# A product of halves split once more: three of seven sub-products in seven half-width ones, mask stores on another queue, the stage in written order

## The chip, the cores and the metric

The kernel runs on one core of a Trainium2 chip. The metric is device time in microseconds; times are medians of several runs. The engines are TensorE (PE, with its weight loads shown as PEld), VectorE (DVE), ScalarE (ACT), GpSimd (POOL) and SyncE (SP, which here only issues DMAs). L12 is line 12 of the kernel.

## The reference, cut to what matters

Two graph layers on x (4096 x 512) and adj (4096 x 4096), each added to its input and normalized over the row. The second layer contains the product that is changed:

```python
x = layernorm(x + relu(adj @ (max(sign(x), 0) @ sign(w0).T)))      # layer 0
node_att = softmax(x @ node_w, axis=0)
h = x @ edge_w                                                     # the changed product
e = where(adj > 0, h @ h.T, NEG_BIG)
edge_att = softmax(e, axis=1)
x = layernorm(x + (adj * (node_att * edge_att)) @ (x @ w1) + bias) # layer 1
```

All is float32. Adjacency is symmetric in its pattern, about 1.6% filled, so `adj > 0` is a mask of the score matrix.

## The kernel before, in words

The kernel goes through four large stages: the aggregation of layer 0 (L459, L460, from 55 to 505 us), the product h (505 to 602 us), the scores h h^T with their masks and exponentials, and the aggregation of layer 1 (L1413, L1563). TensorE does their matmuls nearly without a pause.

In the stage of h, x1T holds the normalized rows transposed (512 features on four chunks of 128 partitions, 4096 columns), and the result is hT, laid out in the same way. Both are cut into quarters: two halves of the features (`HK` = 2 chunks each) and two halves of the columns (g and g + `HG`, 512 columns of one block each). So for each of four g a 2 x 2 block product is computed with seven sub-products in place of eight (Strassen's scheme in Winograd's form). Their left operands are sums of quarters of edge_w, made once on GpSimd (`lops`, L480 to 483: s1 to s4); their right operands are x1T's quarters and four differences of them, t1 to t4, made on VectorE (L498, 499, 502, 504), each 128x1024.

`seven` (L90) does one g: each sub-product m is two feature blocks q times two chunks k of 128, four matmul instructions of 128x128 by 128x512 into a PSUM bank per q. A float32 matmul instruction runs as two passes through the array, so TensorE's rows count passes. Six PSUM banks are held, three pairs. The order of sub-products is 0, 5, 4, 6, 1, 3, 2. ScalarE copies the first and fifth out (L113, L127), VectorE adds the others into hT (L116, L122, L123, L131, L135). A scheduler orders these instructions by its own costs in this stage.

Between sub-products `between_h` steps the remaining work of other stages along:

- `late`: the rest of the last node blocks of layer 0, with their Strassen operands for a later stage, written to DRAM by GpSimd's queue (L388 to 414). The last block's normalization (L356 to 367) and its transposes (TensorE L419, copied by ScalarE L420) fall into the first microseconds of the product.
- `rights_h`: the t differences of the next g.
- `premask`: the adjacency's masks. A piece is loaded from adj (SyncE's queue, L345, 128x1024 float32, 512 KB), VectorE turns it into a bfloat16 mask in the same buffer (L339), and GpSimd's queue stores it in DRAM (L340, 256 KB), for the score stage to read. 26 of the pieces are left for this stage. They go through seven buffers (`single`, `ends`, four in `more`, `sums_l`), of which three are left free at a time (`ahead` = 3).

After the product in the code stand the node maximum (VectorE L534), the maximum across partitions (GpSimd L536), its negation, the exponential (ScalarE L540) and the sum across partitions (GpSimd L542). The scheduler moves them to 512 to 523 us. Then the score stage begins: VectorE forms operands from hT (`right`, L874 to 877; `lent` and `slot`, L783 to 796), TensorE multiplies (L745, L806).

Of the kernel before, what the change touches and what calls it, by code (L numbers as in the profile page):

```python
# [11 lines left out]
F32 = mybir.dt.float32  # L12
# [3 lines left out]
ALU = mybir.AluOpType  # L16
AX = mybir.AxisListType

P = 128
# [10 lines left out]
def kernel(  # L30
# [13 lines left out]
    nc = tc.nc  # L44
    N, D = x.shape
# [41 lines left out]

    xw = big.tile([P, NB, D], F32R, name="xw", tag="large")

    def seven(lop, rop, dests, after):  # L90

        K = len(rop(0))
        banks = [[ps_mm.tile([P, W], F32, name="seven", tag="mm") for q in range(2)] for _ in range(3)]

        def multiply(bank, m, first, then):
            for q in range(2):
                for k in range(K):  # L100
                    nc.tensor.matmul(  # L101
                        banks[bank][q],
                        lop(m, q)[k],
                        rop(m)[k],
                        start=(first and k == 0),
                        stop=(k == K - 1),
                        skip_group_check=not first,
                    )
                then(banks[bank][q], q, *dests[q])
                after(None, None)  # L110

        def m1(ps, q, c11, c12, c21, c22):
            nc.scalar.copy(c21, ps)  # L113

        def u2(ps, q, c11, c12, c21, c22):
            nc.vector.tensor_add(c12, c21, ps)  # L116

        def nothing(*_):
            pass

        def u3(ps, q, c11, c12, c21, c22):
            nc.vector.tensor_add(c22, c21, ps)  # L122
            nc.vector.tensor_add(c22, c22, banks[2][q])  # L123
            after(q, 3)

        def m2(ps, q, c11, c12, c21, c22):
            nc.scalar.copy(c11, ps)  # L127
            after(q, 0)

        def m4(ps, q, c11, c12, c21, c22):  # L130
            nc.vector.tensor_add(c21, c21, ps)  # L131
            after(q, 2)

        def m3(ps, q, c11, c12, c21, c22):
            nc.vector.tensor_add(c12, c12, ps)  # L135
            after(q, 1)

        multiply(0, 0, True, m1)
        multiply(1, 5, True, u2)
        multiply(2, 4, True, nothing)  # L140
        multiply(1, 6, False, u3)
        multiply(0, 1, False, m2)
        multiply(1, 3, False, m4)
        multiply(2, 2, False, m3)

    def layernorm(ts_):
        n = len(ts_)
# [11 lines left out]
    with (  # L159
# [65 lines left out]
        def product(g, j):  # L225
            pw = pws[g, j] = ps_mm.tile([P, D], F32, name="pw", tag="mm")
            for k in range(KD):
                nc.tensor.matmul(pw, rights_s[g][:, k, ts(j, P)], bw[:, k, :], start=(k == 0), stop=(k == KD - 1))
                if g == 0 and (not j or k == KD - 1):
                    zeros(2)  # L230
# [97 lines left out]
        bufs = deque([pair[:, 0, :], pair[:, 1, :], single, ends])  # L328
        loaded = deque()

        def premask(queue, left, ahead=2):

            if loaded and (len(bufs) <= ahead or len(pieces) == left):
                (r, j, c), a = loaded.popleft()

                m = a.bitcast(BF16).rearrange("p (c w) -> p c w", c=2)[:, :, :W]
                a_ = a.rearrange("p (c w) -> p c w", c=2)

                tc.keep_in_program_order(nc.vector.tensor_scalar(m, a_, 0.0, NEG_BIG, ALU.is_le, ALU.mult))  # L339
                nc.gpsimd.dma_start(mask_d[r][:, c : c + 2, j, :], m)  # L340
                bufs.append(a)
            if len(pieces) > left:
                r, j, c = pieces.popleft()
                a = bufs.popleft()
                queue.dma_start(a, adj[ts(r * BG + j, P), c * W : (c + 2) * W])  # L345
                loaded.append(((r, j, c), a))
# [83 lines left out]
        with tc.manual_schedule(engines={mybir.EngineType.DVE, mybir.EngineType.Activation}):  # L430
            for n in range(NB):
                b = n // 2 // BG * 2 * BG + n // 2 % BG + n % 2 * BG
                xb = rows.tile([P, D], F32, name="xb", tag="rows")
                nc.sync.dma_start(xb, x[ts(b, P), :])
                if b in early:

                    before = xb, rest(n, b, xb, accs[n], before and before[0])
                    if n == 0:
                        parts.append(before[1])
                    continue  # L440
                acc = ps_mm.tile([P, D], F32, name="acc", tag="mm")
                for half in range(2):
                    at = stream.tile([P, HB, P], F32, name="at", tag="stream")
                    nc.sync.dma_start(at, adj_t[b, :, ts(half, HB), :])

                    for q in range(2):
                        aq = at[:, ts(q, QC), :]
                        hi = sp.tile([P, QC, P], F32R, name="hi", tag="hi")
                        nc.scalar.copy(hi, aq)  # L449
                        lo = sp.tile([P, QC, P], F32R, name="lo", tag="lo")  # L450
                        nc.vector.tensor_sub(lo, aq, hi.bitcast(F32))  # L451
                        if n == 2 and half == 1 and q == 0:
                            parts.append(before[1])
                        step()
                        if half == 1:
                            premask(nc.scalar, 26)
                        for c in range(QC):
                            kb = half * HB + q * QC + c
                            nc.tensor.matmul(acc, hi[:, c, :], xw[:, kb, :], start=(kb == 0), stop=False)  # L459
                            nc.tensor.matmul(acc, lo[:, c, :], xw[:, kb, :], start=False, stop=(kb == NB - 1))  # L460
                parts.append(rest(n, b, xb, acc, before[0]))
                before = xb, None
                if n == NB - 3:
                    assert not loaded
                    bufs.clear()
                    bufs.extend((single, ends))
                    we_s = wp.tile([P, KD, D], F32, name="we_s")
                    nc.sync.dma_start(we_s, edge_w.rearrange("(k p) o -> p k o", p=P))
            while parts:
                step()  # L470
# [12 lines left out]
        nc.gpsimd.tensor_sub(s4, l12, s2)  # L483
        left_h = l11, l12, s4, l22, s1, s2, s3

        more = [stream.tile([P, 2, 2 * W], F32, name="more", tag="stream") for _ in range(2)]
        bufs.extend(m[:, n, :] for m in more for n in range(2))
        bufs.append(sums_l.rearrange("p n f -> p (n f)"))
        for _ in range(4):
            premask(nc.sync, 0, 3)  # L490
        count = [0]
        rights = {}

        def rights_h(g):
            r11, r12 = (x1T[:, :HK, ts(c, W)] for c in (g, g + HG))
            r21, r22 = (x1T[:, HK:, ts(c, W)] for c in (g, g + HG))
            t1, t2 = (sp.tile([P, HK, W], F32, name="t12", tag="hi") for _ in range(2))
            nc.vector.tensor_sub(t1, r12, r11)  # L498
            nc.vector.tensor_sub(t2, r22, t1)
            yield  # L500
            t3, t4 = (sp.tile([P, HK, W], F32, name="t34", tag="lo") for _ in range(2))
            nc.vector.tensor_sub(t3, r22, r12)
            yield
            nc.vector.tensor_sub(t4, r21, t2)
            rights[g] = r11, r21, r22, t4, t1, t2, t3
            yield

        ahead_h = deque(p for g in range(1, HG) for p in [rights_h(g)] * 3)
        for _ in rights_h(0):
            pass  # L510

        def between_h(q, n):
            count[0] += q is None
            if q is None and count[0] > 1:
                next(late[-1], None)
            if q is None and count[0] % 14 in (8, 10, 13) and ahead_h:
                next(ahead_h.popleft())
            if q is None and count[0] > 6 and count[0] % 5 % 2 == 0:
                premask(nc.sync, 0, 3)

        for g in range(HG):
            right_h = rights.pop(g)
            seven(
                lambda m, q: [left_h[m][:, k, ts(q, P)] for k in range(HK)],
                lambda m: [right_h[m][:, k, :] for k in range(HK)],
                [[hT[:, q + f, ts(c, W)] for f in (0, HK) for c in (g, g + HG)] for q in range(2)],
                between_h,
            )

        assert not loaded and not pieces  # L530


    nmax = const.tile([P, 1], F32, name="nmax")
    nc.vector.tensor_reduce(nmax, node_s, AX.X, ALU.max)  # L534
    gmax = const.tile([P, 1], F32, name="gmax")
    nc.gpsimd.partition_all_reduce(gmax, nmax, P, bass_isa.ReduceOp.max)  # L536
    nc.vector.tensor_scalar(gmax, gmax, -1.0, None, ALU.mult)
# [1416 lines left out]
```

## Time and profile before

| | us |
|---|---|
| runs | 1904.31, 1905.71, 1904.44 |
| median | 1904.44 |
| profiled execution | 1903.96 |
| its span | 1902.2 |
| TensorE busy | 1890.8 |
| stage of the changed product | 505.4 to 602.1 |

The profile is of one execution. The span counts from the first to the last instruction; 1.76 us of the execution's time lie around it. Rows name engine, line, operation, and the tiles written and read. [...]

### The profile page before, as it was taken

Reading aid. Unit: us, or ns where it says so; the run is one execution under the profiler, and the core shown is the slowest. Engines: PE = TensorE matmul, PEld = TensorE weight load, DVE = VectorE, ACT = ScalarE, POOL = GpSimd, SP = SyncE. Lnnn points to the kernel's source line nnn. Section 1 sums busy time; section 2 is a strip of 40 time slices with the busy share of each in tenths; the row PEclk is TensorE's granted clock in tenths of the full one; section 3 lists DMA queues with packets and bytes.
Section 4 is the critical chain, followed back from the end, with each engine's and each line's share of the span. In section 5 each row is a group of like instructions: output and inputs, shape, how many; then the busy total and the mean of one; then the engine's idle time right before and its main releaser. Section 6 shows DMA issues by size and latency. Waiting matters only on the chain.

```text
span 1902.2 us, 21262 instructions
## 1 busy us (share of the span) xinstructions
PE 1890.8 (99%) x7054; PEld 1263.4 (66%) x7054; DVE 1527.5 (80%) x2421; ACT 1024.6 (54%) x1669; POOL 314.1 (17%) x449
## 2 busy tenths in 40 slices
PE   9999999999999999999999999999999999999998
PEld 6888888888645656565667556666666666656646
DVE  7777677776877689888896887898879988898947
ACT  6433333333211567666777666665676567667732
POOL 0133132232331111111110111111111101110100
PEclk9999999999999999999999999999999999999999
DMA  9889898898585379577795978878777878787831
GB/s 321 299 322 362 308 339 323 330 353 321 179 295 190 141 267 346 191 259 277 286 334 166 327 279 297 287 288 300 273 278 287 294 270 277 268 318 253 286 114 56
DMA packets 143919, 521.00 MB, mean 274 GB/s; under 512 B 15040, under 2 KB 15040, under 8 KB 136128
## 3 DMA queue, kind: packets, MB, share of 16 engines
q1 hardware_dynamic: 64368, 235.43, 36.7%
q0 software_dynamic: 67632, 248.54, 34.2%
q10 hardware_dynamic: 11808, 35.66, 5.0%
q8 instruction: 56, 0.92, 0.2%
q14 instruction: 55, 0.45, 0.1%
HBM read 397.93 MB, written 121.63 MB: 273 GB/s over the span
## 4 chain that ended last, share of the span: by engine, by line
PE 89%; DVE 7%; ACT 2%; DMA 1%; issue 1%; ACTq 0%; SPq 0%; DVEq 0%
PE bank L1413 33%; PE acc L460 11%; PE acc L459 11%; PE bank L1011 11%; PE seven L101 5%; PE po L1563 4%; PE pt L707 3%; PE bank L806 2%; PE bank L970 2%; PE bank L933 2%; PE bank L745 2%; DVE lent L1182 1%; PE pt L419 1%; DVE slot L1182 1%; PE acc L253 1%
## 5 line engine op out<-in xcount | busy, mean ns | idle before, releaser
L1413 PE MATMUL bank<-lent,lop 128*128 128x256 f32 (+1 forms) x1368 | 433.0, 466 | 1.1 <-DVE lent L1194 0.7
L459 PE MATMUL acc<-xw,hi 128*128 128x512 f32 x960 | 376.4, 392 | 0.0
L460 PE MATMUL acc<-xw,lo 128*128 128x512 f32 x960 | 374.2, 390 | 0.0
L1413 PEld LDWEIGHTS bank<-lent,lop 128*128 128x128 f32 x1368 | 259.3, 190 | 146.1 <-issue 119.9
L1413 PE MATMUL bank<-slot,lop 128*128 128x512 f32 (+1 forms) x928 | 335.4, 508 | 0.4 <-DMA lop<-lop_d 0.2
L1413 PEld LDWEIGHTS bank<-slot,lop 128*128 128x128 f32 x928 | 176.0, 190 | 136.8 <-issue 121.3
L449 ACT CAST hi<-at 128x1024 fp32r<-128x1024 f32 x120 | 126.5, 1054 | 203.2 <-PE acc L459 152.9
L1424 ACT COPY over<-bank 128x512 f32<-128x512 f32 x200 | 116.0, 585 | 198.1 <-PE bank L1413 194.5
L460 PEld LDWEIGHTS acc<-xw,lo 128*128 128x128 f32 x960 | 180.3, 188 | 37.1 <-DVE lo L451 0.3
L459 PEld LDWEIGHTS acc<-xw,hi 128*128 128x128 f32 x960 | 180.3, 188 | 36.8
L451 DVE TENSOR_TENSOR lo<-at,hi 128x1024 fp32r<-128x1024 f32 x120 | 147.8, 1232 | 64.6 <-ACT hi L449 64.1
L678 ACT ACTIVATE line<-line,nmax_c 128x512 f32<-128x512 f32 x160 | 115.2, 726 | 22.4 <-DVE nmax_c L669 22.0
L669 DVE CUSTOM_DVE_ANT_0 line<-lent,slot 128x512 f32<-128x512 bf16 x144 | 93.1, 687 | 9.5 <-ACT slot L708 6.8
L1575 DVE SCALAR_TENSOR_TENSOR xb<-po,f,xb 128x256 f32<-128x256 f32 x84 | 40.3, 481 | 75.0 <-PE po L1563 70.8
L1386 ACT COPY bank<-over 128x512 f32<-128x512 f32 x144 | 86.8, 603 | 0.0
L707 PEld LDWEIGHTS pt<-ident,lent 128*128 128x128 f32 x406 | 50.9, 141 | 36.6 <-issue 24.2
L745 PE MATMUL bank<-hT 128*128 128x512 f32 (+3 forms) x256 | 75.1, 433 | 0.0
L1182 DVE CUSTOM_DVE_ANT_1 lent<-lent,line 128x2048 f32<-128x2048 f32 x32 | 73.0, 2283 | 1.1 <-DMA lent<-s_d 1.1
L708 ACT COPY slot<-pt 128x512 f32<-128x512 f32 (+3 forms) x125 | 68.0, 554 | 10.8 <-PE pt L707 10.8
L420 ACT COPY x1T<-pt 128x512 f32<-128x512 f32 x32 | 18.8, 587 | 101.7 <-PE pt L419 101.7
L1188 ACT ACTIVATE slot<-slot 128x2048 f32<-128x2048 f32 x35 | 67.3, 1924 | 10.8 <-DMA slot<-in_adj_t_dram 10.8
L1182 DVE CUSTOM_DVE_ANT_1 slot<-slot,line 128x2048 f32<-128x2048 f32 x32 | 73.1, 2284 | 0.0
(356 smaller groups left out, 3280.1 us busy)
## 6 DMA issues: line engine op xcount, KB each, us to landing
lop<-lop_d SPq DMA_DIRECT2D x154, 512.0 KB, 4.4
at<-in_adj_t_dram SPq DMA_DIRECT2D x60, 1024.0 KB, 7.3
slot<-in_adj_t_dram POOLq DMA_DIRECT2D x37, 1024.0 KB, 8.1
s_d<-slot POOLq DMA_DIRECT2D x32, 1024.0 KB, 7.6
slot<-s_d POOLq DMA_DIRECT2D x31, 1024.0 KB, 7.4
lent<-s_d POOLq DMA_DIRECT2D x29, 1024.0 KB, 8.2
lent<-in_adj_t_dram POOLq DMA_DIRECT2D x27, 1024.0 KB, 7.6
lent<-in_adj_dram SPq DMA_DIRECT2D x48, 512.0 KB, 6.2
```

The source lines that it names most:

```text
L101: nc.tensor.matmul(banks[bank][q], lop(m, q)[k], rop(m)[k], start=(first and k == 0), stop=(k == K - 1), skip_group_check=not first,)
L449: nc.scalar.copy(hi, aq)
L451: nc.vector.tensor_sub(lo, aq, hi.bitcast(F32))
L459: nc.tensor.matmul(acc, hi[:, c, :], xw[:, kb, :], start=(kb == 0), stop=False)
L460: nc.tensor.matmul(acc, lo[:, c, :], xw[:, kb, :], start=False, stop=(kb == NB - 1))
L678: nc.scalar.activation(line, line, AF.Exp, bias=nmax_c[:, b, c : c + 1], scale=-1.0, accum_out=sum_c[:, b, c : c + 1])
L707: nc.tensor.transpose(pt[:, j, :], src[:, ts(j, P)], ident)
L745: nc.tensor.matmul(pe[:, lo * P :], hT[:, k, ts(A * BG + i, P)], hT[:, k, (B * BG + lo) * P : (B + 1) * W], start=(k == 0), stop=(k == KD ...
L1011: nc.tensor.matmul(ps, left[m][:, k, q, :], right[m][:, k, :], start=(first and k == 0), stop=(k == KD // 2 - 1), skip_group_check=not first,)
L1182: pinned[0](nc.vector._custom_dve(TENSOR_ADD_SAT, out=q, in0=q, in1=m, s0=0.0, s1=-HUGE))
L1413: nc.tensor.matmul(ps, lop[:, k, :], rop[:, k, :], start=start, stop=(k == K - 1), skip_group_check=True)
L1424: nc.scalar.copy(self.to(), self.bank[:, : self.w])
```

## The change

For the first g one of the seven sub-products (5), for the others three (0, 4 and 5), are themselves split into seven products by the same scheme: over the two chunks, the two feature blocks and two halves of 256 columns. Such a sub-product was four matmul instructions of 512 columns and is now seven of 256 (`quarters`). Its operands are made by GpSimd: `inner_left` (four 128x128 sums, once for each of the three left operands) and `inner_right` (four 128x256 sums, for each split sub-product). The partial products meet in PSUM: a small bank `own` (one of the two that the transposes use) holds two of them, ScalarE copies parts into the sub-product's banks and into a scratch tile (five copies of 128x256 for each split), and TensorE accumulates onto these copies; VectorE adds twice 128x256.

TensorE, VectorE and ScalarE follow the written order in this stage (`manual_schedule`). The instructions of split sub-products alternate with each other and with whole ones (`mix`), and the second half of the last sub-product is issued among the next g's first (`over`). The sub-products run in the order 0 and 4, 5 with 1, 2, 6, 3. t1 and t2 of the next g are made earlier than before.

Mask stores go to SyncE's queue, behind which the loads stand; four buffers (`more`) at first and `sums_l` from count 16, one of them left free at a time. The pieces go at counts 4, 5, 7, 12 and from then on at two of three counts; there are 12 counts for each g, 48 in all. `single` and `ends` are no longer mask buffers in this stage, and the two loads into them before it are gone.

The node maximum is taken at count 46; what hangs on it stays behind the product in the code. In the order of the built program, the two `right` subtractions that ran before the end of the stage stand behind it.

The diff, cut to its core:

```diff
-    def seven(lop, rop, dests, after):
+    def seven(lop, rop, dests, after, inner, spare, over):
...
+        def quarters(bank, m, z):
+            left, right = inner[m]
+            own = ps_tr.tile([P, W], F32, name="own", tag="tr")
+            y = own[:, :HD]
+            alone_ = z is None
+            z = own[:, HD:] if alone_ else z
+            (x11, x12), (x21, x22) = ((x[:, :HD], x[:, HD:]) for x in banks[bank])
+            zs = spare()
+
+            def multiply(ps, n, first=False):
+                nc.tensor.matmul(ps, left[n], right[n], start=first, stop=True, skip_group_check=True)
+
+            multiply(y, 0, True)
+            if not alone_:
+                nc.scalar.copy(x11, y)
+            yield
+            multiply(z, 4, not alone_ and bank == 0)
+            if alone_:
+                nc.scalar.copy(x11, y)
+            yield
+            multiply(y, 5)
+            nc.scalar.copy(x12, y)
+            nc.scalar.copy(zs, z)
+            yield
+            multiply(y, 6)
+            nc.scalar.copy(x22, y)
+            nc.scalar.copy(x21, y)
+            yield
+            multiply(x11, 1)
+            yield
+            multiply(x12, 2)
+            nc.vector.tensor_add(x12, x12, zs)
+            yield
+            multiply(x21, 3)
+            nc.vector.tensor_add(x22, x22, zs)
+            yield
...
-        multiply(0, 0, True, m1)
-        multiply(1, 5, True, u2)
-        multiply(2, 4, True, nothing)
-        multiply(1, 6, False, u3)
-        multiply(0, 1, False, m2)
-        multiply(1, 3, False, m4)
-        multiply(2, 2, False, m3)
+        if 0 in inner:
+            z = [banks[1][0][:, h * HD : (h + 1) * HD] for h in range(2)]
+            order = (0, 1, 0, 1, 2, 0, 1, 2, 0, 1, 0, 1, 0, 1, 0, 1)
+            mix(order, quarters(0, 0, z[0]), quarters(2, 4, z[1]), over[0])
+        else:
+            alone(product(0, 0, True, nothing))
+            alone(product(2, 4, True, nothing))
+        for q, (c11, c12, c21, c22) in enumerate(dests):
+            nc.scalar.copy(c21, banks[0][q])
+        for q, (c11, c12, c21, c22) in enumerate(dests):
+            nc.vector.tensor_add(c22, c21, banks[2][q])
+        mix((0, 0, 1, 0, 1, 1, 0, 0, 0, 1, 0), quarters(1, 5, None), product(0, 1, False, m1))
+        for q, (c11, c12, c21, c22) in enumerate(dests):
+            nc.vector.tensor_add(c12, c21, banks[1][q])
+        alone(product(2, 2, False, m2))
+        alone(product(1, 6, False, m6))
+        over[0] = product(1, 3, False, m3)
+        next(over[0])
+        next(over[0])
+        after()
...
-                nc.gpsimd.dma_start(mask_d[r][:, c : c + 2, j, :], m)
+                (to or nc.gpsimd).dma_start(mask_d[r][:, c : c + 2, j, :], m)
...
+        def inner_right(R, *to):
+            r11, r12, r21, r22 = (R[:, k, ts(c, HD)] for k in range(2) for c in range(2))
+            t1, t2, t3, t4 = to
+            nc.gpsimd.tensor_sub(t1, r12, r11)
+            nc.gpsimd.tensor_sub(t2, r22, t1)
+            nc.gpsimd.tensor_sub(t4, r21, t2)
+            nc.gpsimd.tensor_sub(t3, r22, r12)
+            return r11, r21, r22, t4, t1, t2, t3
...
-        bufs.append(sums_l.rearrange("p n f -> p (n f)"))
-        for _ in range(4):
-            premask(nc.sync, 0, 3)
+        for _ in range(3):
+            premask(nc.sync, 0, 1, nc.sync)
...
-            if q is None and count[0] % 14 in (8, 10, 13) and ahead_h:
-                next(ahead_h.popleft())
-            if q is None and count[0] > 6 and count[0] % 5 % 2 == 0:
-                premask(nc.sync, 0, 3)
+            if g + 1 < HG:
+                if n == 4:
+                    rights[g + 1].make(1)
+                    inside(g + 1, 0, rights[g + 1].r11)
+                    inside(g + 1, 4, rights[g + 1].t[1])
+                elif n == 7 + 3 * (not g):
+                    rights[g + 1].make(2)
+                    inside(g + 1, 5, rights[g + 1].t[2])
+                elif n == 11:
+                    rights[g + 1].make(3)
+            if n == 2 and 0 < g:
+                rights[g].make(4)
+            if count[0] == 12 * HG - 2:
+                nc.vector.tensor_reduce(nmax, node_s, AX.X, ALU.max)
+            if count[0] in (4, 5, 7, 12) or count[0] > 12 and count[0] % 3:
+                premask(nc.sync, 0, 1, nc.sync)
...
+        with tc.manual_schedule(engines={mybir.EngineType.DVE, mybir.EngineType.Activation, mybir.EngineType.PE}):
...
-    nmax = const.tile([P, 1], F32, name="nmax")
-    nc.vector.tensor_reduce(nmax, node_s, AX.X, ALU.max)
```

More of the change, by code (lines that the diff above doesn't have):

```diff
@@ L88, with product @@
     xw = big.tile([P, NB, D], F32R, name="xw", tag="large")
-    def seven(lop, rop, dests, after):
+    def seven(lop, rop, dests, after, inner, spare, over):
         K = len(rop(0))
         banks = [[ps_mm.tile([P, W], F32, name="seven", tag="mm") for q in range(2)] for _ in range(3)]
-        def multiply(bank, m, first, then):
+        def product(bank, m, first, then):
             for q in range(2):
+                ps = banks[bank][q]
                 for k in range(K):
                     nc.tensor.matmul(
[L102 to L107, printed above, removed]
-                    )
[L109 to L116, printed above, removed]
+                        ps, lop(m, q)[k], rop(m)[k], start=(first and k == 0), stop=(k == K - 1), skip_group_check=not first
+                    )
+                    if k == K - 1:
+                        then(ps, *dests[q])
+                    yield
[32 more added lines that the diff above has]
+            nc.vector.tensor_add(x22, x22, zs)
+            yield
@@ L118, in nothing, with mix @@
         def nothing(*_):
             pass
[L121 to L126, printed above, removed]
+        def mix(order, *gens):
+            gens = [list_ for list_ in gens]
+            for n, k in enumerate(order):
+                next(gens[k])
+                if n % 4 == 3:
+                    after()
+            for gen in gens:
+                assert next(gen, None) is None
+            if len(order) % 4 > 1:
+                after()
@@ L127, in m2, with alone, m1, m6 @@
+        def alone(gen):
+            for n, _ in enumerate(gen):
+                if n % 2:
+                    after()
+        def m1(ps, c11, c12, c21, c22):
             nc.scalar.copy(c11, ps)
-            after(q, 0)
-        def m4(ps, q, c11, c12, c21, c22):
+        def m6(ps, c11, c12, c21, c22):
+            nc.vector.tensor_add(c22, c22, ps)
+        def m3(ps, c11, c12, c21, c22):
             nc.vector.tensor_add(c21, c21, ps)
-            after(q, 2)
-        def m3(ps, q, c11, c12, c21, c22):
+        def m2(ps, c11, c12, c21, c22):
@@ L135, in m3 @@
             nc.vector.tensor_add(c12, c12, ps)
-            after(q, 1)
-        multiply(0, 0, True, m1)
-        multiply(1, 5, True, u2)
-        multiply(2, 4, True, nothing)
-        multiply(1, 6, False, u3)
-        multiply(0, 1, False, m2)
-        multiply(1, 3, False, m4)
-        multiply(2, 2, False, m3)
+        if 0 in inner:
[5 more added lines that the diff above has]
+            alone(product(2, 4, True, nothing))
@@ L146, in layernorm @@
+        over[0] = product(1, 3, False, m3)
+        next(over[0])
+        next(over[0])
+        after()
     def layernorm(ts_):
@@ L329, with premask @@
         loaded = deque()
-        def premask(queue, left, ahead=2):
+        def premask(queue, left, ahead=2, to=None):
             if loaded and (len(bufs) <= ahead or len(pieces) == left):
@@ L465 @@
                     bufs.clear()
-                    bufs.extend((single, ends))
                     we_s = wp.tile([P, KD, D], F32, name="we_s")
@@ L484, with inner_left @@
         left_h = l11, l12, s4, l22, s1, s2, s3
+        def inner_left(L, to):
+            l11, l21, l12, l22 = (L[:, k, ts(f, P)] for k in range(2) for f in range(2))
+            s1, s2, s3, s4 = (to[:, n, :] for n in range(4))
+            tc.keep_in_program_order(nc.gpsimd.tensor_add(s1, l21, l22))
+            nc.gpsimd.tensor_sub(s2, s1, l11)
+            nc.gpsimd.tensor_sub(s3, l11, l21)
+            tc.keep_in_program_order(nc.gpsimd.tensor_sub(s4, l12, s2))
+            return l11, l12, s4, l22, s1, s2, s3
@@ new lines, in inner_right, with row_halves @@
+        def inner_right(R, *to):
[6 more added lines that the diff above has]
+            return r11, r21, r22, t4, t1, t2, t3
+        def row_halves():
+            x = rows.tile([P, D], F32, name="right_i", tag="rows")
+            return [x[:, ts(n, HD)] for n in range(2)]
@@ L486 @@
+        ends_i = wp.tile([P, 4, HD], F32, name="ends_i", tag="ends")
+        to_i = {0: [ends_i[:, n, :] for n in range(4)]}
+        mixed = wp.tile([P, 4 * P + 2 * HD], F32, name="mixed", tag="quarter", bufs=2)
+        lefts_i = {5: inner_left(s2, mixed[:, : 4 * P].rearrange("p (n f) -> p n f", f=P))}
+        inners = [{} for _ in range(HG)]
         more = [stream.tile([P, 2, 2 * W], F32, name="more", tag="stream") for _ in range(2)]
         bufs.extend(m[:, n, :] for m in more for n in range(2))
-        bufs.append(sums_l.rearrange("p n f -> p (n f)"))
@@ L489 @@
-        for _ in range(4):
-            premask(nc.sync, 0, 3)
+        for _ in range(3):
+            premask(nc.sync, 0, 1, nc.sync)
         count = [0]
[L492 to L514, printed above, removed]
-                next(late[-1], None)
-            if q is None and count[0] % 14 in (8, 10, 13) and ahead_h:
-                next(ahead_h.popleft())
-            if q is None and count[0] > 6 and count[0] % 5 % 2 == 0:
-                premask(nc.sync, 0, 3)
[L521 to L528, printed above, removed]
+        over = [None]
@@ new lines, with __init__, make, of @@
+        nmax = const.tile([P, 1], F32, name="nmax")
+        class Rights:
+            def __init__(self, g):
+                self.r11, self.r12 = (x1T[:, :HK, ts(c, W)] for c in (g, g + HG))
+                self.r21, self.r22 = (x1T[:, HK:, ts(c, W)] for c in (g, g + HG))
+                self.t = {}
+            def make(self, n):
+                tag = "hi" if n < 3 else "lo"
+                t = self.t[n] = sp.tile([P, HK, W], F32, name="t12" if n < 3 else "t34", tag=tag)
+                a, b = {
+                    1: (self.r12, self.r11),
+                    2: (self.r22, self.t.get(1)),
+                    3: (self.r22, self.r12),
+                    4: (self.r21, self.t.get(2)),
+                }[n]
+                nc.vector.tensor_sub(t, a, b)
+            def of(self, m):
+                return (self.r11, self.r21, self.r22)[m] if m < 3 else self.t[4 if m == 3 else m - 3]
@@ new lines, with inside @@
+        rights = [Rights(g) for g in range(HG)]
+        for n in (1, 2, 3, 4):
+            rights[0].make(n)
+        to_i[5] = row_halves() + row_halves()
+        inners[0][5] = lefts_i[5], inner_right(rights[0].t[2], *to_i[5])
+        to_i[4] = [mixed[:, 4 * P + n * HD : 4 * P + (n + 1) * HD] for n in range(2)] + row_halves()
+        zs_ = deque((wp.tile([P, HD], F32, name="z_s", tag="scr"), wp.tile([P, HD], F32, name="z_s", tag="warm")))
+        def inside(g, m, R):
+            inners[g][m] = lefts_i[m], inner_right(R, *to_i[m])
@@ new lines, in between_h @@
+        def between_h():
+            count[0] += 1
+            g, n = divmod(count[0], 12)
+            if count[0] > 6:
+                next(late[-1], None)
+            if count[0] == 16:
+                assert next(late[-1], None) is None
+                bufs.append(sums_l.rearrange("p n f -> p (n f)"))
+            if count[0] == 1:
+                for m, x, tag in ((0, l11, "nw_b"), (4, s1, "bias_b")):
+                    to = wp.tile([P, 4, P], F32, name="left_i", tag=tag)
+                    lefts_i[m] = inner_left(x, to)
+            if g + 1 < HG:
[14 more added lines that the diff above has]
+                premask(nc.sync, 0, 1, nc.sync)
@@ new lines @@
+        with tc.manual_schedule(engines={mybir.EngineType.DVE, mybir.EngineType.Activation, mybir.EngineType.PE}):
+            for g in range(HG):
+                right_h = rights[g]
+                seven(
+                    lambda m, q: [left_h[m][:, k, ts(q, P)] for k in range(HK)],
+                    lambda m, r=right_h: [r.of(m)[:, k, :] for k in range(HK)],
+                    [[hT[:, q + f, ts(c, W)] for f in (0, HK) for c in (g, g + HG)] for q in range(2)],
+                    between_h,
+                    inners[g],
+                    lambda: zs_.rotate() or zs_[0],
+                    over,
+                )
+            for _ in over[0]:
+                pass
```

## The prediction

> **What bounds the kernel now.** I read the page first, then the chain of waits around the stage, then windows of 12 us, then what the stage's own matmuls waited for. The page:
>
> ```profile
> PE 1890.8 (99%) x7054; PEld 1263.4 (66%) x7054; DVE 1527.5 (80%) x2421; ACT 1024.6 (54%) x1669; POOL 314.1 (17%) x449
> ```
>
> TensorE is busy for all but 1902.2 − 1890.8 = 11.4 us of the span, so only less matmul work can help, and whatever makes TensorE wait costs in full. The chain of waits, from 495 to 640 us:
>
> ```profile
> 505.37 4.29 PE seven L101 x10
> 509.78 0.63 PE pt L419 x4
> 510.41 88.42 PE seven L101 x206
> 598.92 0.54 issue
> 599.46 1.22 DVE right L874
> ```
>
> The columns are start, length, what and how many. The product runs from 505.4 to 602.1 us with one interruption, the four transposes of the last node block. The chain leaves TensorE at 598.9 only because the next stage's first operands hang on VectorE. Windows (busy time of PE, PEld, DVE, ACT, POOL, then granted clock, DMA share, GB/s):
>
> ```profile
> 517.00:529.00 12.00, 12.00 (x29) 5.32 (x28) 11.32 (x22) 2.87 (x5) 6.59 (x9) 1.00 0.40 122
> 541.00:553.00 12.00, 12.00 (x29) 5.32 (x28) 9.12 (x13) 1.17 (x2) 2.18 (x3) 1.00 0.95 354
> 589.00:602.00 13.00, 13.00 (x31) 5.70 (x30) 7.09 (x10) 1.17 (x2) 1.28 (x3) 1.00 0.06 20
> 602.00:615.00 13.00, 13.00 (x55) 8.84 (x54) 13.00 (x31) 3.42 (x9) 0.00 (x0) 1.00 0.84 322
> ```
>
> PE is full in every one, at the full clock. VectorE is nearly full early in the stage (11.32 of 12), has room later, and is full without a gap for 13 us after it. The mask traffic is squeezed into 525 to 585 us. 28 weight loads in 12.00 us give 0.4286 us a pass; each matmul instruction is two passes, 0.857 us.
>
> **Part 1, the product itself.** Before, 4 × 7 × 2 × 2 = 112 matmul instructions, 112 × 0.857 = 96.0 us. After, the first g splits one product and the others three: 72 full instructions and 10 × 7 = 70 of half the columns. The price of a half comes from a later stage that has both widths:
>
> ```profile
> 1540.94 1.03 PE L1563 MATMUL po<-over 128*128 128x256 f32 x4
> 1541.81 1.03 PE L1413 MATMUL bank<-slot,lop 128*128 128x256 f32 x4
> 1542.67 1.89 PE L1413 MATMUL bank<-lent,lop 128*128 128x256 f32 x8
> 1544.40 1.03 PE L1413 MATMUL bank<-slot,lop 128*128 128x256 f32 x4
> ```
>
> From 1540.94 to 1545.26 (where the next row starts) there are 20 passes, 0.216 us each, half of 0.43; the weight load, 0.190 us, still fits below, with 26 ns to spare. So 72 × 0.857 + 70 × 0.432 = 61.7 + 30.2 = 91.9 us: **−4.1 us**, 0.21% of the run. That is all that the change can bring; 0.2% (3.8 us, about what a measurement of this kernel can tell from no change) is passed only if nearly nothing is lost.
>
> **Part 2, what it adds on the other engines.** ScalarE gets 10 × 5 = 50 copies of 128x256, 0.36 us each: 18 us against 1.17 of 12 busy, covered. Inside a split product the second use of a half bank waits for the copy of the first (0.36 us); other products' matmuls, 0.43 to 0.86 us each, lie between, so nothing, or 0.36 us plus a semaphore once per split (4 us over ten) without that cover; I take 0.2. VectorE gets 20 PSUM adds of 128x256 at 0.42 (8.4 us); the 40 of 128x512 remain. Per g it then carries 10 × 0.68 + 6 × 0.42 + 4 × 1.22 + 6.5 masks × 0.69 = 18.7 us of about 23: enough, if nothing stretches it.
>
> GpSimd gets 40 adds of 128x256 and 12 of 128x128. The four operand sums before the stage are 128x512 and took 1.30 to 1.48 us, so about 0.7 and 0.37: 32 us, against 26 mask stores × 0.73 = 19 us taken off its queue. It has room: 30 of 125 us was busy. But these adds are not free for VectorE. Just before the stage, under GpSimd's four sums (484.6 to 492.7):
>
> ```profile
> 484.43 0.42 DVE L407 TENSOR_TENSOR sums_l<-xb 128x256 f32<-128x256 f32 x1
> 484.76 1.51 DVE L408 TENSOR_TENSOR sums_l<-xb 128x256 f32<-128x256 f32 x1
> 486.30 1.41 DVE L409 TENSOR_TENSOR sums_l<-sums_l,xb 128x256 f32<-128x256 f32 x1
> 487.75 1.39 DVE L410 TENSOR_TENSOR sums_l<-xb,sums_l 128x256 f32<-128x256 f32 x1
> 491.74 2.09 DVE L451 TENSOR_TENSOR lo<-at,hi 128x1024 fp32r<-128x1024 f32 x1
> ```
>
> The same 128x256 add took 0.42 alone and 1.4 to 1.5 beside GpSimd; L451 2.09 against 1.23. Four GpSimd sums cost VectorE 1.09 + 0.99 + 0.97 + 0.86 = 3.9 us: 0.98 each, so an estimated 0.49 for one of half the size. The operations hit have two inputs in SBUF, as the t subtractions have; the stage's PSUM adds have one. Whether masks suffer the trace doesn't show. With t work and masks 4 × 1.22 + 6.5 × 0.69 = 9.4 of 23 us, about 0.4 of GpSimd's adds meet one: 40 × 0.49 × 0.4 = 8 us of VectorE time, 2 per g, against 4 spare. On average it fits; but it comes in bursts of up to eight GpSimd adds (up to 4 us), just where the next g's first products need t1, t2 and the banks. VectorE is in order: behind the stretched subtraction queue the c22 and c12 adds, and TensorE's m1 waits for a ScalarE copy that waits for these. Bounds: nothing (slack swallows it) to 8 us less 4 × 0.3. There are three changes of g; I take about 0.4 us at each: **+1.2**.
>
> [...] With masks exempt the sum would lose about half of the 1.2.
>
> **Part 3, mask stores on SyncE.** 26 pieces are left for the stage, each a 512 KB load and a 256 KB store. Now a load queues on SP behind a store that waits for VectorE's mask, and each load waits until the store of the call before has landed: two pieces cost one store landing plus an issue of 0.33 us. There are 24 calls from count 12 to 47, 35 steps of 1.92 us (92 us over 48): 2.8 to 2.9 us apart. So the loop keeps up as long as a store lands within 2 × 2.87 − 0.33 = 5.4 us. Before, stores landed in 5.4 us (median) under a DMA share of 0.8 to 0.95, but 2.54 us in the quiet end of the stage (579 to 595). Spread evenly, 26 × 768 KB = 20 MB over 85 us are 240 GB/s against 354 at a share of 0.95: about 0.64. Between 2.5 and 5.4 I take 4: **0**.
>
> **Part 4, node maximum late.** The reduction (0.18 us), the library load before GpSimd's all-reduce (GpSimd idled 6.2 us for it before), the exponential with its table load (1.28 us) and the sum leave the start of the stage, where VectorE is fullest, and come 3 us before its end. VectorE's negation and reciprocal wait for GpSimd with the last m6 and m3 adds queued behind, and the next stage behind these. The two `right` subtractions that ran before 602 (L874, L875: 2.3 us) now come after. Into the 13 full microseconds of VectorE after the stage this pushes 2 to 6 us; TensorE has queued matmuls there (it lost 0.13 us in the next 15). Bounds 0 to 3: **+0.4**. At the start, the last transposes (0.9 us wait before) share VectorE with GpSimd's first eight adds: 0 to 0.8, **+0.3**.
>
> **Sum.** −4.1 + 0.2 + 1.2 + 0 + 0.4 + 0.3 = −2.0 us. The profiled execution took 1903.96 us (span 1902.2 and 1.76 around it), 0.48 below the median; applied to the median 1904.44 this gives **1902.4 us**. Own range: 1900.7 (losses 0.4) to 1904.6.
>
> **Rivals.**
> Full gain: GpSimd's bursts fall into VectorE's slack and the start of the next stage stays covered; −4.1 to −4.4, 1900.0 to 1900.6. For it: PE waited under 1 us in the old stage and VectorE has 4 us per g free. Against it: the stretched rows above.
>
> Slower, the SP loop: load and store share one queue, so a store also stands behind the load issued before it; loads landed in 4.4 to 8.0 us. If a store then takes 6.3 us (the old queue's maximum), pieces come every (6.3 + 0.33)/2 = 3.3 us, 24 × (3.3 − 2.87) = 10.6 us late at the end, less 3.3 us that three loads ahead cover (3 × 2.87 − 5.3): masks make VectorE wait 7 us, and TensorE with it: −2.0 + 7 = +5, **1909.4**. It decides from 5.4 us of landing. Against: the traffic is thinner. For: the old median is exactly at the limit.
>
> Slower, the late softmax: if the library load holds GpSimd for its 6.2 us with VectorE waiting, the last adds and the next stage's VectorE work come 6 us later; beyond the covered part +3 to +6 on −2.4 (the sum without its 0.4 for this): about 1905 to 1908.5. Against: GpSimd's last adds are issued at count 31 of 48, so in the 29 us before count 46 it can load ahead, if nothing holds the load.
>
> **How the numbers follow.** Forecast 0.36, full gain 0.28, SP loop 0.27, late softmax 0.09. Faster by over 0.2% (under 1900.63): the full gain, and a sliver of the forecast, 0.30. Slower by over 0.2% (over 1908.25): most of the SP loop and the worst of the softmax, and of their sum, 0.32. Within 0.2%: the rest, 0.38. The range 1899.8 to 1911 leaves out the tail of the SP loop (landings above 6.6 us) and little else.
>
> **What would show it.** Right: 72 full instructions at L99 and 70 halves at L116 (two passes each), a stage of 93 to 95 us, t subtractions of 1.7 to 2.5 us beside GpSimd's adds, PE idle of 0.3 to 1 us at changes of g, named VectorE or ScalarE. Full gain: no such idle. SP loop: mask instructions ended by DMA waits and stores landing in over 5.4 us. Softmax: VectorE idle over 2 us for GpSimd around the last adds. My forecast is wrong if TensorE's idle lies elsewhere than at changes of g, or if half-width passes cost over 0.216 us.

## The result, and the profile after

The changed kernel is slower: a median of 1912.74 us (six runs, 1910.38 to 1914.68) against 1904.38, by 0.4%: a ratio of 1.0041 with an interval of 1.0028 to 1.0054. The profiled execution took 1910.48 us, its span is 1908.7.

The page's first part, answering to the line shown of before:

```profile
PE 1889.5 (99%) x7114; PEld 1275.2 (67%) x7114; DVE 1542.8 (81%) x2441; ACT 1041.0 (55%) x1719; POOL 340.2 (18%) x475
```

TensorE is hardly less busy, though it has 4 us less to do, and its idle time has grown from 11.4 to 19.2 us. The stage, counted to the next stage's first matmul, now runs from 505.2 to 610.5 us, 105.3 us where it was 96.9. A pass of 512 columns has a row of 592 ns there, but the next one starts 429 ns after it; for 256 columns it is 379 and 215 ns. The rows of TensorE that start after a wait, from the timeline (start, length, what, and in brackets the idle time and what ended it):

```profile
510.36 0.63 PE L468 MATMUL pt<-ident,xb 128*128 128x128 f32 x4 [0.69 <-DVE xb L411]
527.51 1.98 PE L99 MATMUL seven<-t,we_s 128*128 128x512 f32 x4 [0.62 <-DVE hT L166]
538.52 1.12 PE L99 MATMUL seven<-x1T,we_s 128*128 128x512 f32 x2 [0.39 <-ACT hT L182]
571.97 3.70 PE L99 MATMUL seven<-t,lops 128*128 128x512 f32 x8 [1.19 <-DVE hT L187]
579.28 1.12 PE L99 MATMUL seven<-t,we_s 128*128 128x512 f32 x2 [0.17 <-DVE hT L166]
589.80 1.74 PE L99 MATMUL seven<-x1T,we_s 128*128 128x512 f32 x2 [3.35 <-ACT hT L182]
604.73 1.98 PE L99 MATMUL seven<-t,we_s 128*128 128x512 f32 x4 [0.51 <-DVE hT L166]
608.66 1.98 PE L99 MATMUL seven<-t,we_s 128*128 128x512 f32 x4 [1.95 <-DVE hT L166]
```

That is 8.9 us. Each names VectorE or a ScalarE copy, which is where one looks next: what was VectorE doing? Its waits in the stage, and in the same window the waits of SyncE's queue (what waited for what, total, times, longest):

```profile
DVE more L388 <- DMA more<-in_adj_dram: 10.8, 5, 3.2
DVE sums_l L388 <- DMA sums_l<-in_adj_dram: 5.6, 3, 2.8
```

```profile
SPq L394 <- DMA mask_d<-more: 47.9, 13, 4.7
SPq L389 <- DVE more L388: 17.9, 5, 15.5
SPq L394 <- DMA mask_d<-sums_l: 12.0, 3, 4.7
```

VectorE, in order, stood 16.4 us at the head of its queue with a mask whose adjacency had not arrived, and the PSUM adds that TensorE needed stood behind it. Loads had not been issued, because SyncE's queue waited 60 us in all for mask stores to land. That sum alone doesn't show a loss, as an experiment below has nearly as much of it. The chain of waits says it in order:

```profile
554.49 1.02 DVE more L388
555.51 4.77 DMA mask_d<-more
560.30 4.39 DMA more<-in_adj_dram
565.30 0.93 issue
567.88 5.63 DMA mask_d<-more
573.52 4.32 DMA more<-in_adj_dram
577.93 0.69 DVE more L388
579.00 4.48 DMA mask_d<-sums_l
583.54 4.53 DMA sums_l<-in_adj_dram
588.70 0.77 DVE seven L137 x2
```

From 554 us the end is no longer set by matmuls but by store, load, store, load, one behind the other. In the chain of before this stretch was one row, 88.42 us of TensorE.

Last, the clock (times, then busy time of PE, PEld, DVE, ACT, POOL, granted clock, DMA share, GB/s):

```profile
586.00:589.00 3.00, 0.44 (x3) 0.04 (x1) 0.91 (x2) 0.00 (x0) 0.00 (x0) 1.00 0.71 252
589.00:592.00 3.00, 2.20 (x4) 1.16 (x5) 1.12 (x4) 1.45 (x3) 0.00 (x0) 0.70 0.66 168
592.00:595.00 3.00, 3.00 (x7) 1.52 (x7) 1.65 (x3) 1.23 (x3) 0.00 (x0) 0.73 0.97 350
```

After the pause of 3.35 us the mean granted clock was 0.70 and 0.73 in two windows; in a narrower one, 590.2 to 593.5 us, it was 0.50. The eight passes from 589.80 to 594.60 took 4.80 us, and the same eight of the g before, from 561.56 to 564.60, took 3.04: about 1.8 us on top of the pause.

### The profile page after: what moved, and what is told of

Its sections match the earlier page's. It is cut to its first block, busy times and chain, and to the rows that moved or that the text cites. A ratio compares the mean times of both kernels' runs of the same rounds, so it can differ in the third digit from the quotient of the medians.

```text
span 1908.7 us, 21547 instructions
## 1 busy us (share of the span) xinstructions
PE 1889.5 (99%) x7114; PEld 1275.2 (67%) x7114; DVE 1542.8 (81%) x2441; ACT 1041.0 (55%) x1719; POOL 340.2 (18%) x475
## 4 chain that ended last, share of the span: by engine, by line
PE 84%; DVE 7%; DMA 4%; ACT 2%; issue 1%; POOL 0%; SPq 0%; ACTq 0%; DVEq 0%; POOLq 0%
PE bank L1528 33%; PE acc L508 11%; PE acc L509 11%; PE bank L1126 10%; PE po L1678 4%; PE pt L822 2%; PE bank L921 2%; PE bank L860 2%; PE bank L1048 2%; PE bank L1085 2%; DVE lent L1297 1%; DMA more<-in_adj_dram 1%; DVE slot L1297 1%; PE pt L468 1%; PE acc L302 1%
```

## The experiments

Theory A: the mask loop on SyncE's queue. Theory B: GpSimd's sums stretch VectorE's work. Theory C: the late node softmax. Ratios are to the kernel before, on the same chip. The diffs are cut to one of the lines changed; where `premask` is called twice, both calls are changed alike.

### Mask stores back on GpSimd's queue (e1_pool)

```diff
-                premask(nc.sync, 0, 1, nc.sync)
+                premask(nc.sync, 0, 1)
```

> The changed kernel with its mask stores back on GpSimd's queue, nothing else. Theory A (the mask loop on SyncE's queue: a load waits for a store to land, that store landed 4.4 to 5.8 us behind a load on the same queue, and the next store stands behind the waiting load): VectorE's waits for mask loads (16.4 us in the changed kernel) go to under 2 us, TensorE's waits of 9 us go to under 2, the stage is 93 to 96 us, the time 1900.5 to 1903. Theory B (GpSimd's operand sums stretch VectorE's subtractions and masks, and TensorE waits for these): the stretching stays, and GpSimd has 26 stores of 0.73 us more in its order; 1910 to 1914 or more. Theory C (the node softmax at the end): 1909 to 1914, only its waits at 604 to 609 us matter and these stay.

Measured: 1899.52 us against 1904.11, ratio 0.9976 (0.9966 to 0.9986). VectorE waits for no mask load. All of TensorE's waits in the stage and after it, to 640 us:

```profile
PE pt L468 <- DVE xb L411: 0.7, 1, 0.7
```

The stage is 93.7 us. Theory A stands, B and C fall: GpSimd carries its sums and the 26 stores, and the softmax is as late as in the changed kernel. This version beats both kernels, by 0.24% and 0.7%.

The stores did not land much sooner (those from `more` in 4.5 us, median, against 4.8), and the loads still waited for them:

```profile
SPq L394 <- DMA mask_d<-more: 60.3, 18, 24.3
SPq L394 <- DMA mask_d<-sums_l: 13.4, 3, 5.4
```

Without the one wait of 24.3 us at the start that is 49 us against 60. What is gone is the other half of the loop: no store stands behind a waiting load any more.

### Mask stores on ScalarE's queue (e2_act)

```diff
-                premask(nc.sync, 0, 1, nc.sync)
+                premask(nc.sync, 0, 1, nc.scalar)
```

> The changed kernel with its mask stores on ScalarE's queue, which is in written order with the copies. Theory A: a queue of its own, so a store is not behind a load and lands in 2.1 to 4 us, loads start earlier, 1901 to 1904 (a little over stores on GpSimd's queue, since a store that waits for VectorE's mask holds ScalarE's copies). Theory B: 1910 to 1914. Theory C: 1909 to 1914.

Measured: 1916.1 us, ratio 1.0062 (1.005 to 1.0075); theory A's 1901 to 1904 was missed. ScalarE's waits:

```profile
ACT seven L120 <- DMA mask_d<-more: 19.2, 2, 9.6
ACT seven L120 <- DVE more L388: 12.2, 1, 12.2
ACT hT L182 <- DVE more L388: 10.8, 3, 5.2
```

A store in ScalarE's order holds its copies until VectorE has made the mask, 23 us in the last two rows, and stores are issued within the two waits of the first row, too (four from 553.96 to 561.09 us, ahead of a copy at 561.50). TensorE waits for the copies (L182 6.7 us, L132 3.1, L120 1.7). The stores did not land in the 2.1 to 4 us that were expected of a queue of their own, but in 4.3 (median of those from `more`). So a queue of its own isn't enough: it must be one on which nothing urgent stands behind a store. The run doesn't tell the theories apart, as it brings a wait of its own.

### SyncE in written order, too (e3_written)

```diff
-        with tc.manual_schedule(engines={... mybir.EngineType.PE}):
+        with tc.manual_schedule(engines={... mybir.EngineType.PE, mybir.EngineType.SP}):
```

> The changed kernel with SyncE, too, in written order in the stage, so that store and load alternate strictly, where the scheduler had put some loads ahead of a store and some behind two. Theory A in its strict form (the queue's order matters): each load waits for the store of the call before, and two pieces take one store landing of 4.5 to 5 us and its issue, 2.4 to 2.9 us a piece against 3.7 in the changed kernel: the waits mostly go, 1901 to 1905. Theory A in its loose form (store and load on one queue are enough): still 1907 to 1913. Theories B and C: no change, 1910 to 1914.

Measured: 1901.37 us, ratio 0.9982 (0.9973 to 0.9991). The built programs have the same instructions in the same order on TensorE, VectorE, ScalarE and GpSimd; only the order of loads and stores on SyncE's queue differs, and that is 11 us. In its stage of 94.8 us VectorE waits for no mask load, and TensorE is idle for 1.5 us. The queue in the changed kernel, from the timeline (start, time to issue, what):

```profile
545.18 0.35 SPq L394 DMA_DIRECT2D more<-in_adj_dram  x1
545.62 0.38 SPq L389 DMA_DIRECT2D mask_d<-more  x1
550.27 0.33 SPq L394 DMA_DIRECT2D more<-in_adj_dram  x1
550.69 0.39 SPq L389 DMA_DIRECT2D mask_d<-more  x1
555.09 0.33 SPq L394 DMA_DIRECT2D more<-in_adj_dram  x1
```

and in written order:

```profile
546.03 0.38 SPq L389 DMA_DIRECT2D mask_d<-more  x1
546.46 0.46 SPq L394 DMA_DIRECT2D more<-in_adj_dram  x1
548.54 0.38 SPq L389 DMA_DIRECT2D mask_d<-more  x1
548.97 0.48 SPq L394 DMA_DIRECT2D more<-in_adj_dram  x1
550.34 0.38 SPq L389 DMA_DIRECT2D mask_d<-more  x1
551.91 0.33 SPq L394 DMA_DIRECT2D more<-in_adj_dram  x1
```

In the first, the scheduler had put loads ahead of stores, so that a load stands directly behind the store it waits for: the load at 550.27 starts when the store of 545.62 has landed, and until then nothing else leaves the queue; a piece takes 4.9 us. In the second, a store and a load of the call between them are issued meanwhile; pieces follow at 2.8 us (14 steps from 546.46 to 586.18). The stores themselves land about as late in both (median 4.8 and 4.3 us).

### No buffer left free (e9_behind)

```diff
-                premask(nc.sync, 0, 1, nc.sync)      # in e3_written
+                premask(nc.sync, 0, 0, nc.sync)
```

> The suspected cost turned up: SyncE in written order as in the version that wrote out its order, but no buffer left free, so that every load goes into the buffer whose store stands directly ahead of it on the queue, and waits for that store to land before anything else is issued. One load more runs ahead. Theory A in its strict form (what counts is how many transfers stand between a store and the load that waits for it): one piece per store landing and issue, 4.4 + 0.4 = 4.8 us against the 2.9 that the stage gives, 24 pieces: TensorE 35 to 45 us late, 1930 to 1945. If stores on the same queue as loads are what costs, whatever their order: 1905 to 1913, as in the changed kernel. If neither: 1901, as with the written order alone.

Measured: 1926.98 us, ratio 1.012 (1.0103 to 1.0137). With every load directly behind the store that it waits for, pieces are 5.1 us apart (551.71 to 627.68 for 15). VectorE waited 43 us for loads. The direction and the step per piece are as theory A's strict form said; the time is 3 us below its range. Four loads run ahead at the start, which may be why; that wasn't tested. Of the 25.6 us over e3_written about 19 are TensorE's idle time in the stage (20.3 against 1.5 us); part of the rest goes with a lower granted clock, whose mean over a run was 0.995 to 0.996 here and 0.999 to 1.000 in e3_written. Towards the end of the stage the built order differs a little on TensorE, VectorE and ScalarE as well.

### Two buffers left free (e6_free2)

```diff
-                premask(nc.sync, 0, 1, nc.sync)
+                premask(nc.sync, 0, 2, nc.sync)
```

> The changed kernel, SyncE's queue in the scheduler's order, but two buffers left free instead of one, so that a load goes into the buffer whose store is one call older (and one load fewer runs ahead). Theory A: the load's wait for a landing store mostly goes, and with it the block of the queue: 1901 to 1905; if the load that is missing ahead is what VectorE now waits for, 1905 to 1909. Theory B and C: no change, 1910 to 1914.

Measured: 1910.3 us, ratio 1.003 (1.0018 to 1.0042): a miss. In the scheduler's order the loads again came to stand just behind their stores (545.83 store, 550.50 load, 550.92 store, 555.65 load), so a freer buffer bought little; VectorE waited 14.3 us.

### The kernel before with its stores on SyncE (e5_before_sp)

```diff
-            premask(nc.sync, 0, 3)
+            premask(nc.sync, 0, 3, nc.sync)
```

> The kernel before, with the mask stores of this stage on SyncE's queue, everything else as before (seven buffers, three left free). Theory A needs both the shared queue and few buffers: a load waits here for a store of three calls before, and the load of a piece runs three ahead, so the queue hardly blocks: 1903.5 to 1906. If the shared queue alone is the cause, 1909 or more. Theory B: as before, 1904, since GpSimd has no sums here.

Measured: 1903.98 us, ratio 0.9997 (0.9988 to 1.0006). With seven buffers, three of them free, the same move of the stores costs nothing, though they landed later than the changed kernel's (5.5 us, median of those from `more`) and the scheduler ordered that queue as well.

### What GpSimd's sums cost (e4_few, e7_pool_few)

In both, the right sums of the third and fourth g are left out (the second g's are used again); the second also has its stores on GpSimd's queue.

```diff
+            if g == 1:
+                once[m] = inner_right(R, *to_i[m])
...
-            inners[g][m] = lefts_i[m], inner_right(R, *to_i[m])
+            inners[g][m] = lefts_i[m], (r11, r21, r22) + once[m][3:]
```

> The changed kernel with GpSimd's right operand sums made for the first two g alone; the third and fourth g use those of the second again (24 of 40 sums of 128x256 left out, TensorE's work is the same). Theory A: the loop is as it was, 1909 to 1914, with VectorE's subtractions at 1.22 us in the last two g. Theory B: the waits of the last two g go, which is where most of TensorE's idle time lies: 1902 to 1906. Theory C: 1909 to 1914.

Measured: 1911.75 us, ratio 1.0041 (1.0028 to 1.0053), the changed kernel's time.

> Mask stores on GpSimd's queue, and GpSimd's right sums for the third and fourth g left out (those of the second used again). It prices what GpSimd's sums cost VectorE and TensorE once the mask loop is out of the way. If the stretching costs TensorE nothing there: within 0.6 us of the version with stores on GpSimd's queue, about 1899 to 1900. By the prediction's term (1.2 us for three changes of g, two of them without sums here): 0.8 us faster than that version.

Measured: 1899.30 us, ratio 0.9976 (0.9966 to 0.9986), that of e1_pool to the last digit. No price of theory B shows, with or without the loop. The two ratios alone are known to 0.1% (2 us) only; e1_pool's row above, in which TensorE waits at no change of g, is the sharper answer.

### Everything but the split (e8_nosplit)

```diff
-        mix((0, 0, 1, 0, 1, 1, 0, 0, 0, 1, 0), quarters(1, 5, None), product(0, 1, False, m1))
+        alone(product(1, 5, True, nothing))
+        alone(product(0, 1, False, m1))
```

This diff is cut: products 0 and 4 are whole as well, in the changed order; stores are on GpSimd's queue as in e1_pool.

> Mask stores on GpSimd's queue, written order, late node maximum and even masks as in the changed kernel, but no sub-product split: 112 matmul instructions of 512 columns, no sums on GpSimd in the stage. If the split alone brings the gain (4.1 us of TensorE work): 1903.5 to 1904.5, as before. If the order and the even masks bring something of their own: below 1903.

Measured: 1905.78 us against 1904.59, ratio 1.0007 (0.9998 to 1.0016), a little over what was expected. TensorE waited

```profile
PE seven L99 <- DVE hT L169: 2.4, 3, 0.8
```

once at each change of g, a wait of this version's own order. So e1_pool is 6.3 us faster by the medians (5.9 by the ratios). Net of the idle time in the two stages, 2.5 against 0.7 us, 4.1 to 4.5 are left for the split. The kernel before with its 96.9 us, 0.1 of them idle, gives 3.8 against e1_pool's 93.7. That order, even masks and late softmax bring something of their own doesn't show; with this version's own wait in it, the run can't exclude about 1 us.

## Why the prediction was wrong, step by step

**What bounds the kernel, and part 1** were right: the split takes off 3.8 to 4.5 us of matmul time (4.1 forecast). Half-width passes cost what the later stage had shown, 0.43 us for two. Without the loop, in e1_pool, the time is 4.6 us shorter (2.7 to 6.5 by its interval), that of the rival "full gain"; but only 3.2 us of it lie in the stage (see "Open").

**Part 3 is the step that failed.** It priced the loop at "0": "two pieces cost one store landing plus an issue", so the loop keeps up as long as a store lands within 5.4 us. The landing was estimated well enough (4 us; 4.8 measured, median, under the limit). But the two pieces per landing hold for the order in which store and load are written, and SyncE isn't among the engines that the change puts in written order. In e3_written, which has that order, two transfers stand between a load and the store it waits for, in all 15 loads from 546 to 587 us. In the changed kernel 12 of the 18 loads from 540 to 603 us stand nearer, when each load is matched with the store that landed just before it was issued: three directly behind their store, nine with one transfer between. Where a load stands directly behind, a landing plus an issue buys one piece, not two: 4.9 to 5.1 us against the 2.9 that were needed. Over all, the loads were 3.7 us apart on average (17 steps from 540.1 to 602.9). In place of 0 the built order of the loop cost 11.4 us, by the medians of the changed kernel and e3_written. The prediction used the order of the built program for VectorE, but not for SyncE's queue.

**The rival** of the SP loop named the right place, the queue and the victim, and its 1909.4 us lies 3 us from the result; but its condition, landings above 5.4 us, did not hold for the median: seven of 26 stores took 5.5 to 6.6 us, and in e1_pool those from `sums_l` took 5.6 us (median of four) without harm. So its nearness is luck in part. The range's upper end of 1911 was tied to a landing time, not to an order, and it left out the clock, about 1.8 us. Two slips change little: from count 12 to 47 there are 25 calls, not 24, and the late softmax's sum ends at 1908.0, not 1908.5.

**Part 2.** GpSimd's sums do stretch VectorE's subtractions, as the rows of before had shown. In e1_pool:

```profile
L586 DVE TENSOR_TENSOR t<-x1T x8: 1216/1340/1624, 501.3 to 573.2; 128x1024 f32<-128x1024 f32 x8
L586 DVE TENSOR_TENSOR t<-x1T,t x8: 1210/1222/1676, 504.5 to 579.3; 128x1024 f32<-128x1024 f32 x8
```

(shortest, median and longest in ns; 1.22 us without a neighbour; 1.7 to 2.5 us had been forecast beside one.) But the cost on the path is 0, not 1.2 us: TensorE waits at no change of g. It waits nowhere inside the split products either, for which 0.2 had been set down. The masks were stretched, too: in the changed kernel those in `more` took 839 ns on average, 1.26 us at most, where they had taken 687 on average; the nine masks from 577.93 us on, when GpSimd's last sum (572.67) was over, took 0.68 to 0.70 us. That answers what the prediction left open. Single instructions of the changed kernel show the stretch on both sides: a subtraction begun at 558.05 us, 0.13 us into a GpSimd sum, took 1.68 us, and a sum begun at 535.19, just behind a subtraction (535.16), took 1.77 us where 0.72 is usual. Whether the time is missed is another question.

**Part 4.** The softmax rival is refuted. GpSimd's all-reduce began 0.13 us after the node maximum had ended in the changed kernel, with nothing like the 6.2 us of before in between. What the traces show of the load that the prediction named is two MODIFY_POOL_CONFIG instructions of the all-reduce's line: at 515.8 us before, 6 us ahead of it, and at 573.6 us, 31 us ahead, in the changed kernel. In e1_pool, after 6.1 us in which GpSimd was idle, the all-reduce began only at 599.1 us, 4.6 us after the node maximum, and VectorE waited 1.5 us for the sum, while TensorE waited for neither. The 0.4 us set down for it were not seen. The transposes at the start cost 0.6 us more (0.69 idle instead of 0.11), not 0.3, within the bounds given.

**Open**: from the next stage's first matmul to the start of the last row of matmuls the run took 1293.1 us before, 1291.3 after, 1291.9 in e1_pool and 1293.5 in e3_written, in single executions and with hardly any idle TensorE. So 1 to 2 us come and go there unexplained, and 1.4 of e1_pool's 4.6 us lie outside its stage. The scatter of the changed kernel's runs, 1910.4 to 1914.7, wasn't followed up.

## What to carry to other kernels

On SyncE's queue, too, what stood behind a waiting transfer waited with it (in the changed kernel nothing left SyncE's queue between 546.0 and 550.27 us). Where a load waits for a store, count what stands between the two on the built queue, and how many pieces one landing lets through. When some engines are put into a written order, look at the queues that are left to the scheduler. And give stores that wait for a slow producer a queue on which nothing urgent follows.

## What the runs showed of the hardware

In the changed kernel a 256 KB store landed in 2.1 us on an idle SyncE queue (516.34 us), and in 4.4 to 6.6 us, median 4.7, where it was issued right behind a 512 KB load on the same queue (16 stores); one such store landed 0.7 us after its load (545.18 to 549.57 us for the load, 545.62 to 550.25 for the store). Sharing the queue isn't shown to be the reason: in e2_act, with the stores on ScalarE's queue, those from `more` took 4.3 us, and in e1_pool, on GpSimd's, 4.5 us (medians).

TensorE's granted clock fell after some short pauses: to a mean of 0.57 over 518 to 522 us in e2_act, after a pause of 2.98 us, and of 0.56 over 574 to 577 in e6_free2, after one of only 2.06. After others of 1.95 (the changed kernel) and 2.41 us (e2_act) it stayed at 1.00. So with 2.06 us followed by 0.56 and 2.41 by 1.00, the length of a pause alone didn't tell in these runs whether the clock fell.
